# Spatial self-attention on one core: q and k biases as a row copied by PE, q/k product ahead of the second transposes, and the general path's DMAs on Pool's queue

## The chip, the cores and the metric

The kernel runs on one core of one Trainium2 chip. The time is the device microseconds of one execution; the profile's span is the part of it from the first to the last instruction. Before the change the median of three runs is 2447.41 us (2447.21 to 2447.56); the profiled execution took 2446.75 us and its span is 2445.0 us.

Engines are named as in the profile: PE multiplies matrices (PEld loads its weights), DVE and ACT do element-wise work, Pool (POOL) does a little arithmetic and issues DMAs, SP only issues DMAs. A "q" after a name (SPq, ACTq) is that engine's sequencer.

## What is computed

The input x is (4, 64, 64, 256) in float32: four images, 4096 positions each, 256 channels. Weights are Wq and Wk (256 x 128), Wv (256 x 256), with biases bq, bk (128 each), bv (256) and one scalar gamma.

```python
q = jnp.einsum('bwhc,cd->bwhd', x, Wq) + bq
k = jnp.einsum('bwhc,cd->bwhd', x, Wk) + bk
v = jnp.einsum('bwhc,cd->bwhd', x, Wv) + bv
pq = q.reshape(B, -1, N)          # N = 4096; the reshape mixes positions and channels
pk = k.reshape(B, -1, N)
pv = v.reshape(B, -1, N)
energy = jnp.einsum('bcn,bcm->bnm', pq, pk)
attention = jax.nn.softmax(energy, axis=-1)
out = jnp.einsum('bcm,bnm->bcn', pv, attention)
return gamma * out.reshape(B, W, H, C) + x
```

## The kernel before

The kernel handles one image after another. For each image it first projects, in sixteen blocks `i` of 256 rows of x, and then attends, in 128 steps `u`: sixteen groups `g` of 256 query columns, each against eight blocks `t` of key columns. All values are float32; where precision matters each factor is split into a rounded half and remainders (`halved`, `halve_v`, `halves`), and the products of the halves are summed.

**Projection** (class `Projection`, L102). `load` brings a block of x into one of three buffers by SP's queue (L82). `transposed` turns it on PE, four 128x128 transposes (L122), and ACT copies the result from PSUM to SBUF as `xts` (L128). `qk` multiplies it by the joined weights `wqk_sb`, four products with 256 columns, which the trace shows as eight passes (L135); DVE adds the bias row `bqk_sb`, which stands in all 128 partitions, and writes `qks` (L144). `v` does the same with `wv_sb` (L156), ACT adding the bias `bv` (L165). `project_qk` (L271) then stores q to a scratch tensor `qd` in device memory and writes the halves of k, `f` (ACT L263, then DVE L266), to a scratch tensor `kf`, both by Pool's queue (L275, L279). The attention reads both back (`qr` L303, `k` L314), which makes the reshape of the reference.

**Attention.** `energy` makes two products per key block, `sa` and `sb` (L330), and ACT takes their exponentials (L334). `join`, `upper` and `halves` form the three factors on DVE and ACT; `attend` sums `a` and `bb` over the key blocks (L383). The last column of `vh` and `vl` holds ones, so the sum of the exponentials comes along. `finish` scales, transposes back, adds x and stores by Pool (L420). `finish_last` does it for the last group in a shorter way and stores by SP (L464).

**No maximum is subtracted** before the exponentials. So the kernel checks all sums against bounds at the end (`inside`, L422): PE sums the verdicts of all partitions (`zp`, L449), DVE writes the flag `again` (L460), and all five engines load the flag and branch on it (the `tc.If`, L563). The code inside the If, the **general path**, computes everything once more with the maximum subtracted; for these inputs the flag is 0 and all engines jump over it. Its DMAs are all on SP's queue: loads of x through `load_x`, loads of `xr` (L651) and stores (L661). Pool has no instruction inside it. After the If every engine goes to the closing barriers, which stand under the launch's line in the profile (L688); SP waits there for all queues and engines.

**The order of the work** is written out by hand: inside `manual_schedule` the instructions stand on each engine in the order in which the Python code gives them, and a semaphore wait is put where an instruction needs another engine's or a DMA's result. A DMA counts up one of eight semaphores of its kind (SP's and ACT's share eight, Pool's have eight) taken in turn.

**The start**, around which most of the change lies. Pool makes the identity `ident` (L86) and issues, in this order: bq and bk to all 128 partitions (L91, L92, 64 KB each as written), wv (L94, 256 KB), the two halves of bv (L97) and gamma (L100). SP issues x_0, x_1 and x_2 (256 KB each). ACT loads its table, fills the columns of ones, and issues wq and wk (L223, L224, 128 KB each). PE keeps itself busy with products of ones (`wp`, L197), then follows the order at L486 to L494: transposes of x_0, two more products of ones (L492), transposes of x_1, the q/k product of block 0. The loop after it goes on with block `i`: transposes of block i + 1, q/k product of block i, v product of block i - 1.

PSUM banks for these first blocks are taken in turn from `energies` (four banks of `ps_s`), later from `outputs`. The buffers `qks` are two of the pool `work`, used in turn.

Of the kernel before, what the change touches and what calls it, by code (L numbers as in the profile page):

```python
# [9 lines left out]
F32 = mybir.dt.float32  # L10
# [10 lines left out]
def kernel(  # L21
# [36 lines left out]
    nc = tc.nc  # L58
    B, W, H, C = x.shape
    P = 128  # L60
    N = W * H
    C2 = C // 2
# [13 lines left out]
    xv, ov = columns(x, XB), columns(out, XB)  # L76

    const = ctx.enter_context(tc.tile_pool(name="const", bufs=1))

    def load_x(pool, b, g):  # L80
        t = pool.tile([P, 2, XB], F32, tag="x", name=f"x_{b}_{g}")
        nc.sync.dma_start(t, xv[b, g])  # L82
        return t

    ident = const.tile([P, P], F32, name="ident")
# [1 line left out]
    ones = const.tile([P, P], F32, name="ones")  # L87
    nc.vector.memset(ones, 1.0)
    wqk_sb = const.tile([P, KC, 2 * C2], F32, name="wqk_sb")
    bqk_sb = const.tile([P, 2 * C2], F32, name="bqk_sb")  # L90
    nc.gpsimd.dma_start(bqk_sb[:, :C2], bq.partition_broadcast(P))  # L91
    nc.gpsimd.dma_start(bqk_sb[:, C2:], bk.partition_broadcast(P))  # L92
    wv_sb = const.tile([P, KC, C], F32, name="wv_sb")
    nc.gpsimd.dma_start(wv_sb, wv.rearrange("(k p) e -> p k e", p=P))  # L94
    bv_sb = const.tile([P, KC], F32, name="bv_sb")
    for eh in range(KC):
        nc.gpsimd.dma_start(bv_sb[:, eh : eh + 1], bv[eh * P : (eh + 1) * P].unsqueeze(1))  # L97
    gam2 = const.tile([P, 2], F32, name="gam")
    gam, gam1 = gam2[:, :1], gam2[:, 1:]
    nc.gpsimd.dma_start(gam, gamma.partition_broadcast(P))  # L100

    class Projection:  # L102


        def __init__(self, b, xpool, psum, xt_out, qk_out, v_out):
            self.b, self.xpool, self.psum = b, xpool, psum
            self.xt_out, self.qk_out, self.v_out = xt_out, qk_out, v_out
            self.xs, self.xt = {}, {}

        def load(self, g):  # L110
            if g < NI and g not in self.xs:
                self.xs[g] = load_x(self.xpool, self.b, g)

        def transposed(self, i):

# [78 lines left out]
    with tc.tile_pool(name="ps_w", bufs=1, space=PSUM) as ps_w:  # L194
        wp = ps_w.tile([P, P], F32, name="wp")
# [3 lines left out]
    with ExitStack() as fast:  # L199
        fast.enter_context(tc.manual_schedule())  # L200
        pool = lambda name, bufs, **kw: fast.enter_context(
            tc.tile_pool(name=name, bufs=bufs, **kw)
        )
        xpool, xtpool, qkv = pool("xpool", 3), pool("xtpool", 3), pool("qkv", 1)
# [4 lines left out]
        work = pool("work", 2)  # L209
# [12 lines left out]
            nc.scalar.copy(t[:, :, C : C + 2], ones[:, : 2 * NM].rearrange("p (m t) -> p m t", t=2))  # L222
        nc.scalar.dma_start(wqk_sb[:, :, :C2], wq.rearrange("(k p) d -> p k d", p=P))  # L223
        nc.scalar.dma_start(wqk_sb[:, :, C2:], wk.rearrange("(k p) d -> p k d", p=P))  # L224

        images, qd, kf, units, loads, now = [], {}, {}, {}, {}, {}

# [43 lines left out]
        def project_qk(b, i):  # L271
            images[b].qk(i)
            x = now["qk"]
            for s in range(2):
                nc.gpsimd.dma_start(qd[b, i // 2 + NG // 2 * s][:, i % 2, :], x[:, s, :C2])  # L275
            f = kpool.tile([P, 2, 3, P], F32R, tag="f", name=f"f_{b}_{i}", bufs=2)
            for _ in halved(f, x[:, :, C2:]):
                pass
            nc.gpsimd.dma_start(kf[b, i // 2][:, i % 2], f.rearrange("p s j d -> p s (j d)"))  # L279
# [204 lines left out]
        for b in range(B):  # L484
            pr = images[b]
            if b == 0:  # L486
                now["banks"] = energies
                pr.transposed(0)

                wp = ps_t.tile([P, P], F32, tag="t", name="wp1")  # L490
                for _ in range(2):
                    nc.tensor.matmul(wp, ones, ones, start=True, stop=True)  # L492
                pr.transposed(1)
                project_qk(b, 0)  # L494
            for i in range(1, NI):
                if i == 3:
                    now["banks"] = outputs
                if i + 1 < NI:
                    pr.transposed(i + 1)
                while i == 1 and active:  # L500
                    proceed()
                begin(b, i)
                project_qk(b, i)
                if i == NI - 1:
                    halves(b, 0)
                project_v(b, i - 1)
                proceed()
            project_v(b, NI - 1)
            for u in range(STEPS):
                g, t = divmod(u, NU)  # L510
                ahead = u + LOOK
                if ahead // NU + 1 < NG and ahead % NU == 3:
                    load_q(b, ahead // NU + 1)
                if u == STEPS - NU and b + 1 < B:
                    image(b + 1)
                if u >= STEPS - 3 and b + 1 < B:
                    now["banks"] = energies
                    if u == STEPS - 3:
                        images[b + 1].load(0)
                    elif u == STEPS - 2:  # L520
                        images[b + 1].transposed(0)
                if t == NU - 3:
                    loads[b, "x", g] = load_x(xpool, b, g)


                beside = []
                if ahead // NU + 1 < NG and ahead % NU == 5:
                    beside.append(halve_q(b, ahead // NU + 1))
                if u in (1, 3):
                    beside.append(halve_v(b, NI - 2 + u // 2))  # L530
                for k in range(2):
                    if ahead < STEPS:
                        energy(b, ahead, k)
                    if k == 0:
                        for forms in beside:
                            next(forms)
                    if k == 0 and u + 2 < STEPS:
                        join(b, u + 2)
                        upper(b, u + 2)
                load_k(b, ahead + 2)  # L540
                proceed()
                if u + 1 < STEPS:
                    halves(b, u + 1)
                for forms in beside:
                    next(forms)
                attend(b, u)
                if (b, u) == (B - 1, STEPS - 1):
                    finish_last(b, g, loads.pop((b, "x", g)))
                elif t == NU - 1:
                    start(finish(b, g, now["o"], now["bb"], loads.pop((b, "x", g))))  # L550
                proceed()
            if b + 1 < B:
                proceed()
                images[b + 1].transposed(1)
                proceed()
                project_qk(b + 1, 0)
# [6 lines left out]
    with tc.If(nc.values_load(again[0:1, 0:1]) > 0), ExitStack() as general:  # L563
# [8 lines left out]
        for b in range(B):  # L572
# [8 lines left out]
                lambda i: xtpool.tile([P, KC, 2, P], F32, tag="xt", name=f"gxt_{b}_{i}"),  # L581
                lambda i: ((pq[:, i::NI, :], 0), (pk[:, i::NI, :], C2)),
                lambda i: (pvT[:, 2 * i : 2 * i + 2, :], bv_sb, 1.0),
            )
            for i in range(NI):
                pr.transposed(i)
# [2 lines left out]
            for g in range(NG):  # L589
# [58 lines left out]
                                stop=(2 * t + h == NM - 1),  # L648
                            )
                xr = xpool.tile([P, 2, NB], F32, tag="xr", name=f"gxr_{b}_{g}")  # L650
                nc.sync.dma_start(xr, xg[b, g])  # L651
                nc.vector.tensor_tensor(ssum[:, 0, :], ssum[:, 0, :], ssum[:, 1, :], ALU.add)
                zb = ps_t.tile([P, NB], F32, tag="t", name=f"gzb_{b}_{g}")
                nc.tensor.matmul(zb, ones, ssum[:, 0, :], start=True, stop=True)
# [2 lines left out]
                for s in range(2):  # L657
                    y = work.tile([P, NB], F32, tag="y", name=f"gy_{b}_{g}_{s}")
                    nc.vector.scalar_tensor_tensor(y, r, gam, acc[s], ALU.mult, ALU.mult)
                    nc.vector.tensor_tensor(xr[:, s, :], xr[:, s, :], y, ALU.add)  # L660
                nc.sync.dma_start(og[b, g], xr)  # L661


# [28 lines left out]
```

## Time and profile before

| what | value | from |
|---|---|---|
| time, median of 3 | 2447.41 us | the times |
| span | 2445.0 us | the page's head |
| PE busy | 2434.4 us (100%) | the page, part 1 |
| PEld, DVE, ACT, POOL busy | 98%, 86%, 74%, 17% | the page, part 1 |
| chain that ended last: PE | 99% of the span | the page, part 4 |
| q/k products (L135), v products (L156) | 5% of the chain each | the page, part 4 |
| DMA traffic | 498.92 MB, mean 204 GB/s | the page, part 2 |
| x loads, issue to landing (median) | 3.9 us | the page, part 6 |
| wq, wk | 3.4 and 5.9 us | the answer on DMAs |
| bq, bk as broadcasts | 5.0 and 5.4 us | the answer on DMAs |
| wv | 6.3 us | the page, part 6 |
| bv (two loads), gamma | 5.6 and 5.1 us | the answer on DMAs |
| last output store by SP | 3.5 us | the page, part 6 |

How to read it: an engine's share of busy time says how full it is over the whole span, and a busy PE says little about whether its passes are at their peak. The chain of waits is followed from the last instruction back, so its shares say which engine's speed set the end. Stages are read from the table of windows, which gives the busy time of each engine between two moments; single instructions from the timeline, whose bracket says how long the engine stood idle ahead of an instruction and who released it. Times are microseconds from the span's start.

### The profile page before, as it was taken

The numbers are of one execution on the slowest core, as the hardware profiler recorded it, in microseconds if no ns is written. First come the engines' busy times: TensorE is split into PE (matmuls) and PEld (weight loads), VectorE is DVE, ScalarE is ACT, GpSimd is POOL, SyncE is SP. The second block draws the span as 40 slices with busy tenths as digits, with TensorE's granted clock in tenths as the row PEclk, the third lists the DMA queues.
The fourth block names the chain that finished last, engine by engine and source line by source line (L and its number), as shares of the span: only waits on it lengthen the run. The fifth ranks groups of instructions, "written<-read, shape, count | busy, mean of one in ns | idle before, by whom it ended". The sixth has DMA issues, their size and how long they took to land.

```text
span 2445.0 us, 50042 instructions
## 1 busy us (share of the span) xinstructions
PE 2434.4 (100%) x19988; PEld 2403.8 (98%) x19988; DVE 2100.4 (86%) x2318; ACT 1797.5 (74%) x3201; POOL 425.8 (17%) x781
## 2 busy tenths in 40 slices
PE   9999999999999999999999999999999999999998
PEld 8999999999899999999989999999998999999998
DVE  5988888888698888888869888888886988888887
ACT  5777777777677777777667777777766777777775
POOL 4211111111411111111141111111114111111110
PEclk9999999999999999999999999999999999999999
DMA  7766666665776666666477666666647766666663
GB/s 233 225 201 213 203 207 202 203 214 156 232 225 197 210 204 207 209 197 212 145 241 229 202 201 207 205 209 201 205 143 245 230 204 198 210 204 209 207 202 114
DMA packets 137407, 498.92 MB, mean 204 GB/s; under 512 B 15536, under 2 KB 57264, under 8 KB 137168
## 3 DMA queue, kind: packets, MB, share of 16 engines
q0 software_dynamic: 92320, 453.17, 59.8%
q1 hardware_dynamic: 44304, 42.22, 5.5%
q8 instruction: 160, 2.62, 0.4%
q14 instruction: 79, 0.65, 0.1%
q10 hardware_dynamic: 544, 0.26, 0.0%
HBM read 445.25 MB, written 50.33 MB: 203 GB/s over the span
## 4 chain that ended last, share of the span: by engine, by line
PE 99%; DMA 0%; DVE 0%; SPq 0%; issue 0%
PE a L383 40%; PE bb L383 19%; PE sa L330 19%; PE sb L330 10%; PE qk L135 5%; PE v L156 5%; PE xt L122 1%; PE ot L415 1%; DMA x<-in_x_dram 0%; SPq L82 0%; DVE o L452 0%; PE ot L457 0%; DVE x L463 0%; PE zp L449 0%; DVE r L441 0%
## 5 line engine op out<-in xcount | busy, mean ns | idle before, releaser
L334 ACT ACTIVATE x<-sa 128x512 f32<-128x512 f32 x1024 | 614.2, 600 | 507.6 <-PE sa L330 505.4
L344 DVE TENSOR_TENSOR x<-x,y 128x1024 f32<-128x1024 f32 x512 | 627.0, 1225 | 228.2 <-ACT y L334 228.2
L330 PE MATMUL sa<-q,k 128*128 128x256 f32 x4096 | 733.2, 279 | 0.0
L355 DVE TENSOR_TENSOR l<-x,h 128x1024 fp32r<-128x1024 f32 x512 | 624.0, 1219 | 0.0
L358 DVE SCALAR_TENSOR_TENSOR d<-h,x 128x1024 fp32r<-128x1024 f32 x512 | 624.0, 1219 | 0.0
L330 PEld LDWEIGHTS sa<-q,k 128*128 128x128 f32 x4096 | 617.9, 188 | 0.4
L334 ACT ACTIVATE y<-sb 128x512 f32<-128x512 f32 x1024 | 615.1, 601 | 0.0
L383 PE MATMUL a<-vh,h 128*128 128x258 f32 x4096 | 574.3, 282 | 0.0
L383 PE MATMUL a<-vl,l 128*128 128x258 f32 x4096 | 571.9, 282 | 0.0
L330 PE MATMUL sb<-q,k 128*128 128x256 f32 x2048 | 566.2, 276 | 0.0
L383 PE MATMUL bb<-vd,d 128*128 128x256 f32 x4096 | 556.3, 278 | 0.0
L314 POOL DMA_DIRECT2D k<-kf x512 | 279.8, 546 | 1566.6 <-PE sb L330 1541.7
L349 ACT ACTIVATE h<-x 128x1024 fp32r<-128x1024 f32 x512 | 543.9, 1062 | 9.1 <-DVE x L344 8.4
L383 PEld LDWEIGHTS a<-vl,l 128*128 128x128 f32 x4096 | 524.6, 189 | 0.0
L383 PEld LDWEIGHTS a<-vh,h 128*128 128x128 f32 x4096 | 522.7, 189 | 0.0
L383 PEld LDWEIGHTS bb<-vd,d 128*128 128x128 f32 x4096 | 513.7, 188 | 0.0
L330 PEld LDWEIGHTS sb<-q,k 128*128 128x128 f32 x2048 | 384.9, 188 | 0.1
L135 PE MATMUL qk<-wqk_sb,xts 128*128 128x256 f32 x512 | 121.1, 379 | 0.0
L156 PE MATMUL v<-xts,wv_sb 128*128 128x256 f32 x512 | 120.3, 379 | 0.0
L156 PEld LDWEIGHTS v<-xts,wv_sb 128*128 128x128 f32 x512 | 97.3, 190 | 13.2
L135 PEld LDWEIGHTS qk<-wqk_sb,xts 128*128 128x128 f32 x512 | 92.3, 190 | 10.0
L275 POOL DMA_DIRECT2D qd<-qks x128 | 69.4, 550 | 179.5 <-DVE qks L144 170.3
(60 smaller groups left out, 868.6 us busy)
## 6 DMA issues: line engine op xcount, KB each, us to landing
k<-kf POOLq DMA_DIRECT2D x512, 768.0 KB, 4.7
x<-in_x_dram SPq DMA_DIRECT2D x128, 256.0 KB, 3.9
kf<-f POOLq DMA_DIRECT2D x64, 384.0 KB, 3.7
out_dram<-x POOLq DMA_DIRECT2D x63, 256.0 KB, 2.5
qd<-qks POOLq DMA_DIRECT2D x128, 64.0 KB, 2.9
qr<-qd SPq DMA_DIRECT2D x64, 128.0 KB, 3.6
wv_sb<-in_L_conv_Wv_dram POOLq DMA_DIRECT2D x1, 256.0 KB, 6.3
out_dram<-x SPq DMA_DIRECT2D x1, 256.0 KB, 3.5
```

What stands on the lines that cost most here:

```text
L122: nc.tensor.transpose(tp[:, k, s, :], self.xs[i][:, s, k * P : (k + 1) * P], ident,)
L135: nc.tensor.matmul(qk[:, s, :], self.xt[i][:, k, s, :], wqk_sb[:, k, :], start=(k == 0), stop=(k == KC - 1),)
L156: nc.tensor.matmul(vp[:, eh, :], wv_sb[:, k, eh * P : (eh + 1) * P], self.xt[i][:, k].rearrange("p s a -> p (s a)"), start=(k == 0), stop= ...
L275: nc.gpsimd.dma_start(qd[b, i // 2 + NG // 2 * s][:, i % 2, :], x[:, s, :C2])
L314: nc.gpsimd.dma_start(t.rearrange("p (i s) f d -> p i s (f d)", s=2), kf[b, u % NU])
L330: nc.tensor.matmul(to[:, i], kt[:, 2 * k + i, f, :], q[:, f], start=first, stop=last)
L334: nc.scalar.activation(to[:, 2 * k : 2 * k + 2, :], sp.rearrange("p i j d -> p i (j d)"), AF.Exp, scale=scale,)
L344: nc.vector.tensor_tensor(x, x, y, ALU.mult)
L349: nc.scalar.activation(h, units[b, u], AF.Identity, scale=UPPER)
L355: nc.vector.tensor_tensor(l, x, h.bitcast(F32), ALU.subtract)
L358: nc.vector.scalar_tensor_tensor(d, h.bitcast(F32), 1.0 + E, x, ALU.mult, ALU.subtract)
L383: nc.tensor.matmul(out_, left[:, i, j * P : (j + 1) * P], right[:, m, : out_.shape[1]], start=(t == i == 0 and (left is h or left is d and ...
```

## The change

Three edits, of which two concern the start and one the end.

1. **Biases of q and k.** They are no longer copied to all partitions by DMAs on Pool's queue. ACT's queue loads each as a row into one partition (0.5 KB each, after wq and wk), in a buffer of `qks` (`bqk_row`). PE multiplies a column of ones by the row (`bqk_all`, in the bank of `bb`), which puts the row in all partitions, and DVE copies the result to `bqk_sb`. One of the two products of ones at L492 goes. On Pool's queue bv and gamma now come first and wv last.
2. **Order of the first products.** The q/k product of block 0 comes ahead of the transposes of block 1.
3. **General path.** Its DMAs are issued by Pool instead of SP, so SP has none inside the If. The loads of the fast path stay on SP.

```diff
-    def load_x(pool, b, g):
+    def load_x(pool, b, g, by=nc.sync):
         t = pool.tile([P, 2, XB], F32, tag="x", name=f"x_{b}_{g}")
-        nc.sync.dma_start(t, xv[b, g])
+        by.dma_start(t, xv[b, g])
         return t
...
     bqk_sb = const.tile([P, 2 * C2], F32, name="bqk_sb")
-    nc.gpsimd.dma_start(bqk_sb[:, :C2], bq.partition_broadcast(P))
-    nc.gpsimd.dma_start(bqk_sb[:, C2:], bk.partition_broadcast(P))
     wv_sb = const.tile([P, KC, C], F32, name="wv_sb")
-    nc.gpsimd.dma_start(wv_sb, wv.rearrange("(k p) e -> p k e", p=P))
     bv_sb = const.tile([P, KC], F32, name="bv_sb")
     for eh in range(KC):
         nc.gpsimd.dma_start(bv_sb[:, eh : eh + 1], bv[eh * P : (eh + 1) * P].unsqueeze(1))
     gam2 = const.tile([P, 2], F32, name="gam")
     gam, gam1 = gam2[:, :1], gam2[:, 1:]
     nc.gpsimd.dma_start(gam, gamma.partition_broadcast(P))
+    nc.gpsimd.dma_start(wv_sb, wv.rearrange("(k p) e -> p k e", p=P))
...
+        row = work.tile([P, 2, 2 * C2], F32, tag="qk", name="bqk_row")[:1, 0, :]
+        nc.scalar.dma_start(row[:, :C2], bq.unsqueeze(0))
+        nc.scalar.dma_start(row[:, C2:], bk.unsqueeze(0))
...
                 pr.transposed(0)
 
                 wp = ps_t.tile([P, P], F32, tag="t", name="wp1")
-                for _ in range(2):
-                    nc.tensor.matmul(wp, ones, ones, start=True, stop=True)
+                nc.tensor.matmul(wp, ones, ones, start=True, stop=True)
+                bp = ps_o.tile([P, 2 * C2], F32, tag="bb", name="bqk_all")
+                nc.tensor.matmul(bp, ones[:1, :], row, start=True, stop=True)
+                nc.vector.tensor_copy(bqk_sb, bp)
+                project_qk(b, 0)
                 pr.transposed(1)
-                project_qk(b, 0)
...
                 lambda i: (pvT[:, 2 * i : 2 * i + 2, :], bv_sb, 1.0),
+                nc.gpsimd,
             )
...
-                nc.sync.dma_start(xr, xg[b, g])
+                nc.gpsimd.dma_start(xr, xg[b, g])
...
-                nc.sync.dma_start(og[b, g], xr)
+                nc.gpsimd.dma_start(og[b, g], xr)
```

The class `Projection` takes the issuing engine as an argument and hands it to `load_x`; the fast path leaves it at SP.

More of the change, by code (lines that the diff above doesn't have):

```diff
@@ L100, with __init__ @@
     nc.gpsimd.dma_start(gam, gamma.partition_broadcast(P))
+    nc.gpsimd.dma_start(wv_sb, wv.rearrange("(k p) e -> p k e", p=P))
     class Projection:
-        def __init__(self, b, xpool, psum, xt_out, qk_out, v_out):
-            self.b, self.xpool, self.psum = b, xpool, psum
+        def __init__(self, b, xpool, psum, xt_out, qk_out, v_out, by=nc.sync):
+            self.b, self.xpool, self.psum, self.by = b, xpool, psum, by
             self.xt_out, self.qk_out, self.v_out = xt_out, qk_out, v_out
@@ L111, in load @@
             if g < NI and g not in self.xs:
-                self.xs[g] = load_x(self.xpool, self.b, g)
+                self.xs[g] = load_x(self.xpool, self.b, g, self.by)
         def transposed(self, i):
```

## The prediction

> **What bounds the kernel now.** I read the page's chain first (PE 99% of the span), then cut the span into stages in the table of windows. Columns: window, its length, then busy us (and count) of PE, PEld, DVE, ACT, POOL, then clock, DMA share, GB/s.
>
> ```profile
> 4.40:7.07 2.67, 1.34 (x9) 1.18 (x9) 0.00 (x0) 0.59 (x1) 0.80 (x2) 1.00 0.86 237
> 7.07:2434.20 2427.13, 2427.13 (x19950) 2397.62 (x19951) 2097.11 (x2302) 1794.26 (x3195) 421.58 (x769) 1.00 0.66 205
> 2434.20:2438.10 3.90, 2.62 (x19) 1.91 (x17) 3.17 (x15) 0.95 (x2) 0.00 (x0) 1.00 0.00 0
> 2438.10:2445.00 6.90, 0.00 (x0) 0.00 (x0) 0.00 (x0) 0.00 (x0) 0.00 (x0) 0.55 0.15 50
> ```
>
> From 7.07 to 2434.20 PE has no idle at all: 2427.13 of 2427.13 us. The change removes no PE work there, so it can win only in the first 7.07 us and after 2434.20, where the last 6.90 us hold no arithmetic. Next, the timeline of the start, PE alone (start, duration, line, operation), then ACT alone:
>
> ```profile
> 4.51 0.89 PE L122 MATMUL xt<-ident,x 128*128 128x128 f32 x4
> 5.24 0.61 PE L492 MATMUL wp<-ones 128*128 128x128 f32 x4
> 7.07 0.66 PE L122 MATMUL xt<-ident,x 128*128 128x128 f32 x4 [1.22 <-DMA x<-in_x_dram]
> 7.58 1.97 PE L135 MATMUL qk<-wqk_sb,xts 128*128 128x256 f32 x8
> 9.38 0.60 PE L122 MATMUL xt<-ident,x 128*128 128x128 f32 x4
> ```
> ```profile
> 5.44 0.59 ACT L128 COPY xts<-xt 128x512 f32<-128x512 f32 x1 [3.02 <-PE xt L122]
> 7.76 0.59 ACT L128 COPY xts<-xt 128x512 f32<-128x512 f32 x1 [1.74 <-PE xt L122]
> 10.30 0.42 ACT L263 ACTIVATE f<-qks 128x256 fp32r<-128x256 f32 x1 [1.96 <-DVE qks L144]
> 10.63 0.57 ACT L128 COPY xts<-xt 128x512 f32<-128x512 f32 x1
> ```
>
> PE stands 1.22 us for x_1, though xts_0 has been ready since 5.44 + 0.59 = 6.03; the first q/k product starts at 7.58 and the second at 9.81. Why is x_1 late? Issued at 1.48, it landed 5.55 us later by the chain of waits; x_0 took 3.4. The DMA view of 3.0 to 4.3 us (packets, MB, share of 16 engines' time):
>
> ```profile
> q1 hardware_dynamic: 134, 0.12, 29.9%
> q0 software_dynamic: 15, 0.05, 43.1%
> ```
>
> Of 16 x 1.3 = 20.8 us of engine time, Pool's queue q0 took 9.0 us for 15 packets, 0.60 us each; its head is the two bias broadcasts (64 KB each). A packet of x on q1 took 6.2/134 = 0.046 us. Then the end, by the If's line L563 (engine, operation, count, duration in ns, start):
>
> ```profile
> L563 SPq EVENT_SEMAPHORE  x8: 17/17/17, 2442.3 to 2442.8; - x8
> ...
> L563 POOLq COMPARE_BRANCH  x1: 45/45/45, 2437.2 to 2437.2; - x1
> ...
> L563 PEldq COMPARE_BRANCH  x1: 3770/3770/3770, 2437.7 to 2437.7; - x1
> ...
> L563 SPq COMPARE_BRANCH  x1: 45/45/45, 2439.7 to 2439.7; - x1
> ...
> L563 PEldq EVENT_SEMAPHORE  x1: 51/51/51, 2441.6 to 2441.6; - x1
> ```
>
> SP branches at 2439.7 and does its next thing at 2442.3: 2.6 us. ACT (2437.2 to 2439.9) and DVE (2438.2 to 2441.1) show the same gap, 2.7 and 2.9; PE 3.8. Pool, which has nothing inside the If, is at its final drain at 2437.4, 0.2 us after branching. SP is last: eight waits to 2442.8, twelve more from 2442.9, its drain at 2443.6 (line L688), and the closing barriers take 1.4 us to 2445.0.
>
> **What the Trainium skill says.** "Runtime: NRT & Kernel Launch", Instruction fetch mechanics: a taken branch whose target lies outside the two pages held forces a fetch. The trace agrees: 2.6 to 3.8 us on the four engines that jump over code, 0.2 on the one that doesn't. "DMA: Bandwidth & Descriptors", Queues, rings and completion order: each DMA engine takes the queues in turn, a packet at a time. So a 0.60 us packet delays x and the weights; the window above fits, but shows no packet-by-packet order. "TensorE: Matmul & The Clock Gate", What's actually happening: PE is slow until busy for some 3.4 us; the trace agrees (0.24 us a pass from 1.05, 0.11 from about 5), and that warm-up stays.
>
> **The change, part by part.**
>
> *Broadcasts out, rows in.* Two 64 KB loads go from Pool's queue; 2 x 16 packets of 4 KB, an estimate from their size, at 0.60 us are 19 us of engine time, or 1.2 us of all sixteen. Two rows of 0.5 KB go onto ACT's queue, behind wk (issued 1.51, 0.68 us long), so at about 2.2 and 2.8. The queue's only measure is its own: wq landed 3.4 us after issue, wk 5.9, at 7.4. Bounds for wk in the new kernel: 5.3 (x_0, wq, x_1, wk are 768 KB; at the 300 GB/s of the good stretches 2.5 us from the first packet at 2.25, plus 0.5 to complete) and 7.4 (nothing gained). I take about 6.0, 7.4 less the 1.2 us and a little of the thin traffic after 4.3 us. The rows come with wk, or soon after.
>
> *PE's copy.* One warm-up matmul goes (0.3 us), one 128x256 product comes: two passes of 0.215 (L135: 1.73 us per 8), 0.43 us. The new order is wp, rows' product, qk_0, xt_1, xt_2, qk_1. The product stands ahead of qk_0, so it adds a wait: all of PE is queued behind the rows. If they land by 5.5 it ends near 6.0 and costs nothing, since qk_0 waits for xts_0 until 6.03. DVE's copy of the 128x256 sum, some 0.4 us, is done before qk_0 ends: nothing.
>
> *qk_0 ahead of xt_1.* qk_0 starts at S = 6.03 + 0.1 = 6.15 instead of 7.58, 1.4 us earlier. But it pays back. In the new order ACT holds f_0 ahead of xts_1, and f_0 waits for qk_0's bias add on DVE. From qk_0's start: 1.97 its own, 0.03 + 0.69 DVE, 0.03 to f_0, 0.33 until the next copy starts (10.30 to 10.63), 0.57 that copy, 0.1 to PE: 3.7 us until qk_1, with only xt_1 and xt_2 (0.44 each) to fill the 1.9 us after qk_0. Before, 9.81 - 7.58 = 2.23. So qk_1 starts at 6.15 + 3.7 = 9.87 against 9.81: **the start gives +0.06 us**, nothing. With wk at 7.4 it is 7.5 + 3.7 = 11.2: +1.4.
>
> *Pool's other loads.* wv is issued last, at about 3.4 instead of 2.85; at the 6.3 us it took it lands by 10.2, v_0 needs it at 11.6: nothing. bv and gamma come earlier and are first used at 13.5 (v's bias): nothing.
>
> *General path by Pool.* It isn't run here (again is 0), but SP's code inside the If goes and the compiled program leaves SP only its branches there. So SP's 2.6 us should become Pool's 0.2, and its eight waits go with them. What then ends last? The output store, issued at 2438.00, lands 3.5 us later, at 2441.5, and PE's semaphore is set at 2441.65; SP's final waits include both. Three more waits at 0.06 us and the drain: about 2441.85 against 2443.6: **the end gives -1.75 us**. Pool now jumps over code (2437.2 + 2.7 = 2439.9, five waits, 2440.4): hidden behind PE. No more than 2.1 us can be had, as the store itself stands.
>
> *Steady part.* The waits of all later instructions are on the same producers as before; only semaphore numbers and the parity of the qk work buffers shift. PE is without idle: nothing.
>
> Sum: +0.06 - 1.75 = -1.7; 2447.4 - 1.7 = **2445.7 us** (-0.07%).
>
> **The rivals.**
>
> *A, as above*, with start within +-0.5: 2445.7. Chance 0.55.
>
> *B, wk stays late.* Thin traffic from 4.3 to 5.75 us (100 to 155 GB/s, by quarters) outlasts most of the broadcasts, so something else may hold wk. Start +0.5 to +1.4, end -1.75: 2446.2 to 2447.1, say 2446.8. Chance 0.22.
>
> *C, slower: the rows gate PE and the end wins little.* Small loads behind large ones took 5.1 to 5.8 us here (bv, gamma). A row issued at 2.8 and 5.4 long lands at 8.2; product to 8.7, qk_1 at 12.4: +2.6. With -1.75 that is 2448.3; with PE's fetch slowed by Pool's and an end of -0.5, 2449.5. Against it: bv and gamma were on the broadcasts' queue. Chance 0.13.
>
> *D, the start wins too.* ACT passes xts_1 sooner than the sum says, or x_0 comes earlier: -0.5, and -2.1 at the end: 2444.8. Chance 0.10.
>
> **How the numbers follow.** A is the likeliest: 2445.7. The range takes D's 2444.8 below, and B with the better part of C above, 2447.9; left out are worse cases of C and surprises below D, some 15 in 100. The bound of 0.2% is 4.9 us. The biggest win that the sums allow is 2.6 us, and the worst of C is a loss of 2.1; only a disturbed steady part reaches further. Faster 0.03, same 0.95, slower 0.02.
>
> **What would show it.** Right: SP's drain near 2441.9 less the shift of the start, no gap of 2.5 us after SP's branch, PE's semaphore as last; q0's slow packets gone at 3 to 5 us; qk_0 at about 6.15; PE idle about 0.8 us ahead of qk_1, with xts_1 behind f_0 on ACT; PE without idle afterwards. Wrong: qk_0 waiting beyond 6.5 for wk or the rows, SP still fetching, the barriers waiting for Pool, or idle PE in the middle.

## The result and the profile after

| | before | after |
|---|---|---|
| time, median of 6 runs each | 2447.19 us | 2455.43 us |
| ratio after/before, 95% interval | | 1.0033 [1.0021, 1.0046] |
| span of the profiled run | 2445.0 us | 2453.1 us |
| q/k product of block 0: start, length | 7.58, 1.97 | 7.28, 3.30 |
| q/k product of block 1: start | 9.81 | 12.28 |
| the flag's product (`zp` on PE): start | 2436.08 | 2439.08 |
| from there to the end of the span | 8.92 us | 14.02 us |

The kernel became 8.2 us slower, where 1.7 us less was forecast. The last two rows divide the 8.1 us of span: 3.0 us were lost before the flag's product, 5.1 us behind it. `zp` is a good mark to divide at, since the same few instructions precede it in both kernels. Its piece of the chain of waits (start, us, what), before and after:

```profile
2436.08 0.37 PE zp L449 x2
2439.08 0.37 PE zp L451 x2
```

The windows of the kernel after, laid as those of before (window, length, busy us and count of PE, PEld, DVE, ACT, POOL, clock, DMA share, GB/s):

```profile
4.40:7.07 2.67, 1.24 (x8) 0.98 (x8) 0.00 (x0) 0.58 (x1) 0.22 (x1) 1.00 1.01 325
7.07:20.00 12.93, 12.47 (x57) 10.41 (x56) 5.22 (x10) 4.17 (x10) 3.69 (x8) 0.87 0.48 155
20.00:2437.20 2417.20, 2416.92 (x19898) 2388.47 (x19896) 2091.41 (x2293) 1788.58 (x3186) 416.42 (x761) 1.00 0.65 205
2437.20:2441.10 3.90, 2.62 (x19) 1.91 (x17) 3.16 (x15) 0.95 (x2) 0.00 (x0) 1.00 0.00 0
2441.10:2453.10 12.00, 0.00 (x0) 0.00 (x0) 0.00 (x0) 0.00 (x0) 0.00 (x0) 0.52 0.09 29
```

Three things are to be seen. The stretch without arithmetic at the end grew from 6.90 to 12.00 us. From 7.07 to 20.00 PE's granted clock has a mean of 0.87, where it was 1.00. And the middle is nearly as it was: PE idles 0.28 us in 2417.20.

**The start.** PE's timeline of the kernel after (start, duration, line, operation; the bracket is idle time and its releaser), then ACT's:

```profile
4.50 0.63 PE L120 MATMUL xt<-ident,x 128*128 128x128 f32 x4
4.97 0.39 PE L493 MATMUL wp<-ones 128*128 128x128 f32 x2
6.68 0.67 PE L495 MATMUL bqk_all<-bqk_row,ones 1*128 1x256 f32 x2 [1.33 <-DMA bqk_row<-in_L_conv_bk_dram]
7.28 3.30 PE L133 MATMUL qk<-wqk_sb,xts 128*128 128x256 f32 x8
10.37 1.46 PE L120 MATMUL xt<-ident,x 128*128 128x128 f32 x8
12.28 1.99 PE L133 MATMUL qk<-wqk_sb,xts 128*128 128x256 f32 x8 [0.46 <-ACT xts L126]
```
```profile
5.17 0.58 ACT L126 COPY xts<-xt 128x512 f32<-128x512 f32 x1 [2.75 <-PE xt L120]
11.34 0.42 ACT L265 ACTIVATE f<-qks 128x256 fp32r<-128x256 f32 x1 [5.59 <-DVE qks L142]
11.66 1.05 ACT L126 COPY xts<-xt 128x512 f32<-128x512 f32 x2
```

`xts_0` is ready at 5.75, even earlier than assumed, and wk has landed (4.9 us after its issue, at 6.4) when it is wanted. But PE waits 1.33 us for the row of bk. Two things are behind the loss. First, the row: the chain of waits of the kernel after, in order of time, ends its first leg with it:

```profile
2.96 3.59 DMA bqk_row<-in_L_conv_bk_dram
6.55 0.14 issue
6.68 0.67 PE bqk_all L495 x2
```

A load of 0.5 KB takes 3.59 us; it was issued last, behind x_0, wq, x_1 and wk (an experiment below puts it first). The traffic of 3.0 to 4.3 us by queue (packets, MB, share of 16 engines' time) shows that this isn't the broadcasts' doing any more:

```profile
q1 hardware_dynamic: 178, 0.17, 40.8%
q0 software_dynamic: 22, 0.00, 1.3%
```

Pool's queue had 43.1% of this time and now has 1.3%; between 4.40 and 7.07 the loads flow at 325 GB/s instead of 237, and x_1 no longer makes PE wait. The removal did what it was for. The second thing is the q/k product itself, which takes 3.30 us instead of 1.97. Windows of half a microsecond of the kernel after show why (the clock is the third figure from the end):

```profile
7.00:7.50 0.50, 0.50 (x3) 0.22 (x2) 0.11 (x1) 0.00 (x0) 0.03 (x2) 1.00 1.01 330
7.50:8.00 0.50, 0.50 (x3) 0.45 (x3) 0.31 (x1) 0.00 (x0) 0.20 (x1) 0.81 0.41 131
8.00:8.50 0.50, 0.50 (x3) 0.41 (x2) 0.00 (x0) 0.00 (x0) 0.00 (x0) 0.50 0.03 8
...
11.00:11.50 0.50, 0.50 (x6) 0.50 (x5) 0.31 (x1) 0.16 (x1) 0.00 (x0) 0.78 0.00 0
```

A mean of 0.81 over half a microsecond puts the fall to half at about 7.8, and 0.78 the return at about 11.2: some 3.4 us at half speed, just as the first product runs.

**The end.** The If's line in the kernel after (L567; engine, operation, count, ns, start), then the closing line of the launch (L693; DRAIN and EVENT_SEMAPHORE with min/median/max ns and the first and last start), then the closing line of the kernel before (L688). DRAIN and INC_SWDGE_SEM are the profile's names; no statement of kernel.py asks for either here.

```profile
L567 POOLq EVENT_SEMAPHORE  x4: 17/43/43, 2443.5 to 2443.8; - x4
...
L567 POOLq COMPARE_BRANCH  x1: 45/45/45, 2440.2 to 2440.2; - x1
...
L567 SPq COMPARE_BRANCH  x1: 50/50/50, 2442.7 to 2442.7; - x1
...
L567 POOLq INC_SWDGE_SEM  x1: 1787/1787/1787, 2443.8 to 2443.8; - x1
```
```profile
L693 SPq EVENT_SEMAPHORE  x14: 17/28/28, 2445.6 to 2453.0; - x14
L693 POOLq DRAIN  x3: 46/107/6602, 2445.7 to 2452.8; - x3
L693 SPq DRAIN  x3: 7/7/7, 2446.3 to 2452.5; - x3
```
```profile
L688 POOLq DRAIN  x3: 46/107/6683, 2437.4 to 2444.7; - x3
L688 SPq DRAIN  x3: 7/7/13, 2443.6 to 2444.4; - x3
```

Read the drains together. In the kernel before Pool's first drain starts at 2437.4 and takes 6.683 us, to 2444.1; SP's is at 2443.6. So Pool ended last already, by 0.5 us, and the barriers led to 2445.0. In the kernel after Pool branches at 2440.2, jumps over the code of the general path (3.3 us until its four waits at 2443.5), runs an INC_SWDGE_SEM of 1.787 us that was not there before, and only then, at 2445.7, starts the drain, which takes 6.602 us again, to 2452.3. SP is at its drain at 2446.3, 6.0 us before that.

Counted from the flag's product, SP comes to its drain after 7.2 us, where it took 7.5 before. Why so little, if it has no code to jump over any more? It branches at 2442.7, but its closing waits begin only at 2445.6, which is when Pool's INC_SWDGE_SEM ends (2443.8 + 1.787); the view of waits puts the 2.8 us between down to a DMA of Pool's queue. In the later versions with the general path on Pool the two times agree as well (2447.1 and 2447.2 where INC_SWDGE_SEM is long again), so SP most likely waits for that instruction.

### The profile page after: what moved, and what is told of

Its sections match the earlier page's. It is cut to its first block, busy times and chain, and to the rows that moved or that the text cites. A ratio compares the mean times of both kernels' runs of the same rounds, so it can differ in the third digit from the quotient of the medians.

```text
span 2453.1 us, 50041 instructions
## 1 busy us (share of the span) xinstructions
PE 2436.6 (99%) x19988; PEld 2404.8 (98%) x19988; DVE 2100.0 (86%) x2319; ACT 1796.0 (73%) x3201; POOL 423.5 (17%) x779
## 4 chain that ended last, share of the span: by engine, by line
PE 98%; ACT 0%; DMA 0%; issue 0%; DVE 0%; POOL 0%; ACTq 0%; POOLq 0%; DVEq 0%
PE a L385 40%; PE bb L385 19%; PE sa L332 19%; PE sb L332 9%; PE qk L133 4%; PE v L154 4%; PE ot L417 1%; PE xt L120 1%; DMA kf<-f 0%; ACT v L163 0%; DMA bqk_row<-in_L_conv_bk_dram 0%; DVE qks L142 0%; ACT vh L294 0%; ACT f L265 0%; DVE f L268 0%
```

## The experiments

The theory after this reading: Pool's closing drain has a fixed length from where it starts and sets the end, so every delay of it is paid in full; and at the start the rows gate PE and the clock drops in the stall. Rivals: the end's loss belongs to Pool's far branch alone; the drain waits for something that other engines do; the new order costs the start by itself. The chips of the experiments ran the kernel before at 2449.5 to 2449.8 us, with more spread (2447.3 to 2452.6) than the first (2446.7 to 2447.6), so every version's time is compared with the kernel before on the same chip. The kernel before was profiled on the first chip only, and each version once. "End" is from the flag's product to the end of the span, as in the table (before: 8.92 us).

### The edits apart

```diff
# general path by Pool, in the kernel before (and x's loads in the If, by an argument)
-                nc.sync.dma_start(xr, xg[b, g])
+                nc.gpsimd.dma_start(xr, xg[b, g])
...
-                nc.sync.dma_start(og[b, g], xr)
+                nc.gpsimd.dma_start(og[b, g], xr)
# start only: the changed kernel with these two, and x's loads in the If, on nc.sync
# general path by ACT: as the first, with nc.scalar
```

> The kernel before with the general path's DMAs moved to Pool, nothing else. Theory 1 (Pool's closing drain takes a fixed 6.6 us wherever it starts, and the skip path now puts a far branch and a 1.8 us INC_SWDGE_SEM ahead of it): the drain starts near 2442.7 instead of 2437.4, span +5.1 us, time about 2452.3. Theory 2 (Pool's drain merely waits for the other engines, and the loss of the changed kernel at the end comes from something that its start brings): SP's saved branch shows, time about 2445.5; with theory 2 the drain's 6.6 us would shrink.

> The changed kernel with the general path's DMAs back on SP: the start's edits alone. If the two losses are independent: the end as in the kernel before (10.8 us from PE's last product for attend to the span's end), the start +2.5 to 3.0 us, time about 2449.9. If the end's loss needs the start's edits: about 2455.

> The kernel before with the general path's DMAs on ACT's queue: SP has nothing inside the If, and Pool has nothing either. Theory 1 (the fixed drain of Pool set the end of the kernel before too: 2437.4 + 6.68 = 2444.1): span unchanged within 0.3 us, time about 2447.0, although SP's drain comes near 2441.9. Rival, as the prediction had it (SP's branch and eight waits set the end): -1.75 us, time about 2445.4.

General path on Pool alone: 2455.94 us against 2449.68, 1.0025 [1.0016, 1.0035], end 13.43 us. Pool's drain starts 5.9 us after the flag's product (2441.27) and is as long as before:

```profile
L689 POOLq DRAIN  x3: 46/107/6683, 2447.2 to 2454.4; - x3
```

This one edit loses some 6.3 us on that chip, of which the profiles put 13.43 - 8.92 = 4.5 at the end. The rest lies ahead of the flag's product, where nothing was edited: x_1 and wk came later (a first product at 10.12, 3.75 long). In the three versions that keep the broadcasts and have the general path on Pool wk landed 7.7 to 8.5 us after its issue, in the eight others with broadcasts 5.9 to 7.4; what the edit has to do with it stays open.

Start alone: 2450.96, 1.0002 [0.9993, 1.0011], end 9.03; its rows made PE wait 2.3 us and its first product took 3.78. So the 3.0 us of the first chip don't show in this comparison, because the kernel before is itself over 2 us slower here.

General path on ACT: 2449.82, 1.0000 [0.9991, 1.0009], end 8.85. This is the test of the forecast's gain. SP branched at 2442.6 and did its first wait at 2442.8, so its gap of 2.6 us did become 0.2, as forecast, and yet nothing was gained. Its closing line says why:

```profile
L689 POOLq DRAIN  x3: 46/107/6683, 2440.3 to 2447.5; - x3
L689 SPq DRAIN  x3: 7/7/7, 2445.4 to 2447.2; - x3
```

Pool's drain, 2440.3 + 6.7 = 2447.0, ends 1.6 us after SP's began.

### Is the drain's length fixed?

```diff
# the last output store by Pool, in the kernel before
-            nc.sync.dma_start(ov[b, g], xr)
+            nc.gpsimd.dma_start(ov[b, g], xr)
```

> The kernel before with the last output store (L464) issued by Pool instead of SP, nothing else. Pool can then load the flag only after the store is issued, about 2.1 us later than before. Theory 1 (Pool's closing drain takes a fixed 6.6 us and sets the end): the end moves by the same 2.1 us, time +2.1 us. Theory 2 (the drain ends when the others arrive): the end unchanged, since SP's path gets shorter, not longer. If the drain grows beyond 6.7 us with a store in flight: more than +2.1.

The store delays Pool's drain, and moves work off SP. Measured: 2450.81 us against 2449.66, 1.0006 [0.9997, 1.0015], in time inconclusive; end 10.56 us, 1.64 more than before. The closing line of this version:

```profile
L688 POOLq DRAIN  x3: 46/107/6769, 2440.0 to 2447.3; - x3
L688 SPq DRAIN  x3: 7/7/13, 2443.0 to 2447.0; - x3
```

SP, the last of the other engines, is at its drain at 2443.0, 3.8 us before Pool's long one ends, so that drain doesn't simply end when the others arrive. Pool's drain started 2.96 us after the flag's product instead of 1.32, 1.6 later (2.1 was expected), and the end moved by the same 1.6. Six to seven microseconds that follow their start wherever it is put.

The length isn't quite the same in all versions, and the differences go with the edits: 6.602 us wherever Pool doesn't issue the two broadcasts (the kernel after and the start's edits alone, for example), 6.683 wherever it does (the kernel before, the general path on Pool or on ACT), 6.769 here, with one store more. So the length seems to go with what Pool was given to issue, even 2430 us earlier; what the drain does in that time no view shows.

### Paying the drain early

```diff
                 if (b, u) == (B - 1, STEPS - 1):
+                    nc.gpsimd.drain()
                     finish_last(b, g, loads.pop((b, "x", g)))
```

One version has this with the general path on ACT, one is the changed kernel with this line only.

> The kernel before with a drain of Pool right after its last DMA (near 2421 us, 15 us ahead of the flag) and the general path's DMAs on ACT. Theory 1 (the drain is a settling of Pool's DMA queue, paid once, and then it closes the span): the early drain takes 6.6 us under PE's work, the closing one 0.1 to 0.2 us, and SP's path becomes the last: from PE's product for the flag to the span's end 7.8 us instead of 8.9, time -1.1 us. Rival (the closing drain costs 6.6 us whatever went before): end unchanged.

> The changed kernel as it is, general path on Pool, with a drain of Pool right after its last DMA. Theory (the 6.6 us belong to the DMAs issued before, not to the semaphore increments of the skip path): the closing drain is short, and the end is Pool's far branch and INC_SWDGE_SEM, then the barriers: about 7.8 to 8.3 us from the flag's product instead of 14.0, time -6 us against the changed kernel. Rival (INC_SWDGE_SEM makes a drain long again): end still 13.4 to 14.0 us.

On ACT: 2449.89 against 2449.48, 1.0002 [0.9993, 1.0010], end 8.45, 0.65 more than expected (in the last barrier step PE came to its second drain only at 2446.6, 1.6 us after SP's last). The changed kernel: 2448.05, 0.9995 [0.9986, 1.0003], end 6.25 instead of 14.02, and below the 7.8 to 8.3 that were expected. The early drain's line, the If's and the closing line of the changed kernel with it:

```profile
L552 POOLq DRAIN  x1: 7321/7321/7321, 2419.5 to 2419.5; - x1
```
```profile
L568 POOLq INC_SWDGE_SEM  x1: 181/181/181, 2444.2 to 2444.2; - x1
```
```profile
L694 POOLq DRAIN  x3: 34/51/107, 2444.4 to 2446.0; - x3
```

The long drain lies at 2419.5, where PE has work for another 20 us. After it INC_SWDGE_SEM takes 181 ns instead of 1787, and the closing drains 34 to 107 ns instead of 6602: 7.8 us go from the end, and the time is within the noise that of the kernel before. Pool's far branch is still there (2441.2, its waits at 2443.9), so that alone wasn't the loss.

### The start: rows, order, clock

```diff
# warm: the start's edits with seven products of ones instead of one
-                nc.tensor.matmul(wp, ones, ones, start=True, stop=True)
+                for _ in range(7):
+                    nc.tensor.matmul(wp, ones, ones, start=True, stop=True)
# order only: the kernel before with
-                pr.transposed(1)
                 project_qk(b, 0)
+                pr.transposed(1)
# rows only: the start's edits with the old order
# rows first: the start's edits with the rows issued ahead of wq and wk
```

> The start's edits alone, as in the run before this, with seven products of ones ahead of the rows' product instead of one (six more, 0.22 us each at full clock, which fill PE's 1.3 us wait for the rows). If PE's idle stretch took its clock down: qk_0 takes 1.97 instead of 3.30 us and qk_1 starts 1.3 us earlier, time about 2448.6. If the slow qk_0 has another cause (the weights still landing, PSUM): qk_0 stays at 3.3 us and the time at about 2449.9 or a little more.

> The kernel before with the first q/k product ahead of the transposes of block 1; biases as broadcasts, general path on SP. Theory (the order pays back on ACT what it wins, and wk, held up by the broadcasts and by x_1 and x_2, gates qk_0): PE stands idle from xt_0 until wk lands, near 7.5 to 9, so one long idle stretch instead of x_1's; qk_1 starts 3.7 us after qk_0, later than in the kernel before by 1 to 2 us[...]. Rival (the order by itself is a gain and the rows spoil it): qk_1 earlier than before.

> The start's edits without the new order: rows' product, then the transposes of block 1, then qk_0; general path on SP. Theory (the rows land last of all early loads and PE stands behind them): PE idle from 5.4 until the rows land at 6.5 to 7.4; then xt_1 without a wait, qk_0 0.5 us later, qk_1 2.2 us after qk_0 with no wait for xts_1: against the start's edits together qk_1 comes 1.0 us earlier (no 1.5 us of payback, 0.5 us for xt_1). Rival (the payback of the order is nothing on the chip): qk_1 0.4 us later than with the order.

> The start's edits, general path on SP, with the two rows ahead of wq and wk on ACT's queue instead of behind them. Theory (the rows are late only because they queue behind 256 KB of weights in a saturated DMA): rows' product near 5.0 to 5.5 without a wait, then qk_0 waits for wk, which is issued 1.2 us later and lands at about 7 to 8: PE's idle stretch only moves from the rows to wk, qk_1 within 0.5 us of where it was. Rival (the rows alone were the gate): qk_0 at about 6.2, qk_1 at about 9.9.

| version | first q/k product: start, length | second: start | time, ratio |
|---|---|---|---|
| start alone | 8.67, 3.78 | 14.15 | 2450.96, 1.0002 [0.9993, 1.0011] |
| warm | 7.51, 1.99 | 11.21 | 2449.45, 1.0000 [0.9991, 1.0009] |
| order only | 9.00, 3.75 | 14.46 | 2451.05, 1.0006 [0.9998, 1.0015] |
| rows only | 8.81, 3.62 | 13.08 | 2449.41, 0.9998 [0.9989, 1.0007] |
| rows first | 7.30, 3.65 | 12.65 | 2450.16, 1.0002 [0.9994, 1.0011] |

The ratios settle nothing here; the timelines do. PE's timeline of the warm version:

```profile
5.23 1.73 PE L494 MATMUL wp<-ones 128*128 128x128 f32 x14
6.89 0.69 PE L496 MATMUL bqk_all<-bqk_row,ones 1*128 1x256 f32 x2
7.51 1.99 PE L133 MATMUL qk<-wqk_sb,xts 128*128 128x256 f32 x8
11.21 1.99 PE L133 MATMUL qk<-wqk_sb,xts 128*128 128x256 f32 x8 [0.83 <-ACT xts L126]
```

With the wait filled by products whose result nobody reads, the clock stays at 1.00 and the product takes 1.99 us. Its 12 runs also lie closer (2448.3 to 2450.0) than the 12 of "start alone" (2448.3 to 2451.7). So the stall, by way of the clock, is what lengthened it. From one q/k product to the next it is 11.21 - 7.51 = 3.7 us, to the tenth what the forecast worked out for the new order at full clock. "Rows first" moves the wait: the rows' product runs at 5.12 without one, and the next line of PE's timeline reads

```profile
7.30 3.65 PE L133 MATMUL qk<-wqk_sb,xts 128*128 128x256 f32 x8 [1.48 <-DMA wqk_sb<-in_L_conv_Wk_dram]
```

Whichever load is last gates PE, and the clock falls either way. "Start alone" and "rows only" differ in the order, and both ran this stretch at half speed: from the first product to the second 5.5 and 4.3 us, so the payback of the new order costs 1.2 there, by one profile of each. "Order only" is gated by wk, for 3.53 us, and is no earlier for the new order. In "rows only" the record of the clock shows 1.00 throughout, yet a transpose or a product of ones took at least 421 ns from PE's first to the one at 12.9, where "start alone" shows 275 at 4.9: in that execution PE did not come to full speed before 12.9, and the length of the passes is the safer sign.

### A fill in the kernel before, and versions built from the findings

```diff
# fill: the kernel before with
-                for _ in range(2):
+                for _ in range(8):
                     nc.tensor.matmul(wp, ones, ones, start=True, stop=True)
# all, ACT: rows, old order, eight products of ones, early drain, general path on ACT
# all, Pool: the same with the general path on Pool
```

> The kernel before with eight products of ones instead of two in PE's wait for x_1 (L492), nothing else. If PE's idle stretch costs a window at half clock in part of the runs: qk_0 takes 1.9 us always, the slow part of the runs is gone, median 1 to 1.7 us below the kernel before on a chip where that has slow runs, nothing on one where it has none. If the spread has another cause: no change, or +0.3 us where x_1 lands before the products end.

> Rows of the biases by PE, eight products of ones while they come, the order of the kernel before (x_1's transposes, then qk_0), general path's DMAs on ACT, Pool's drain early. If the effects add: qk_1 at about 10.2 with the clock never down, end 7.8 us from the flag's product: 2 to 3 us below the kernel before on the same chip. If the rows' gate eats what the clock wins: -1.1 us.

> The changed kernel with the old order of the first products, eight products of ones instead of one, and the early drain: as the version with the general path on ACT, but on Pool. Theory: end of 6.3 us, start at full clock (first q/k product about 8.4 us, 1.9 us long, second 10.5), time about 1.2 us below the version with ACT, some 0.15% below the kernel before. Rival (ends do not add to starts): no better than that version, 0.10% below the kernel before.

Fill: 2447.94 us against 2449.48, 0.9995 [0.9987, 1.0004]; its 13 runs lie within 1.4 us, the 41 of before beside it within 4.6. Since the fill takes 1.5 us off the median, the kernel before probably has the slow clock in most of its runs on these chips. All, ACT: 2446.85, 0.9990 [0.9981, 0.9998], end 7.44. All, Pool, on another chip: 2446.18 against 2449.78, 0.9985 [0.9979, 0.9992], end 6.43. It is 0.15% below the kernel before, clear of the noise, and so below both kernels. PE's timeline of its start:

```profile
7.26 0.69 PE L496 MATMUL bqk_all<-bqk_row,ones 1*128 1x256 f32 x2
8.38 1.89 PE L133 MATMUL qk<-wqk_sb,xts 128*128 128x256 f32 x8
```

No wait ahead of the rows' product, and a first product of 1.89 us.

### What the third edit is worth once the drain is paid

```diff
# drain, SP: the kernel before with the early drain
# drain, Pool: the same with the general path on Pool
# each again with the fill of eight products of ones
```

> The kernel before with Pool's drain put ahead of the last block's finishing, and nothing else; the general path stays on SP. From the start of the flag's product on PE to the end of the span: theory (Pool's closing drain is a fixed 6.6 us that hides the worth of everything else at the end): with it gone SP's own drain is last, 7.5 us after the flag's product as in the kernel before, plus 0.9 us of barriers: 8.4 us, 0.5 us less than before. Rival (where the general path stands does not matter once the drain is early): 6.3 us, as in the changed kernel with the early drain.

> The same early drain in the kernel before, with the general path's DMAs by Pool, and nothing of the start. Theory (the third edit removes SP's far branch and eight waits, and what it adds on Pool is short once the drain is paid): 6.3 us from the flag's product to the end, about 2.1 us less than with the path on SP, and time 2.1 us lower than that kernel. Rival (the better end of the changed kernel with early drain came from its start): about 8.4 us, no difference.

> The kernel before with eight products of ones instead of two at the start, the early drain, and the general path by Pool; no rows, old order. It differs from the early drain with the path on Pool only by the six products, which also shift where PE's later code stands. Theory (the 3.2 us that PE took there between its last wait inside the If and its drain is a fetch of code, and goes when PE's code is shifted): end of 6.3 to 6.6 us from the flag's product. Rival (that stall belongs to the path on Pool without the rows): 9.6 us again. Start in both at full clock: first q/k product about 8.4 us, 1.9 us long. Against the best version so far it tells whether the rows are needed: theory that fill and drain are enough, 0.1 to 0.15% below the kernel before.

> The same with the general path on SP. Theory (the third edit removes SP's fetch and eight waits, about 2 us, once the drain is early): end of 8.4 to 9.0 us, time about 2 us above the version with the path on Pool. Rival (the third edit is worth nothing): the same time as that version.

| version | end | time, ratio |
|---|---|---|
| drain, SP | 8.95 us | 2449.98, 1.0002 [0.9993, 1.0010] |
| drain, Pool | 9.65 us | 2451.38, 1.0007 [0.9998, 1.0015] |
| fill, drain, SP | 8.60 us | 2447.86, 0.9992 [0.9984, 1.0000] |
| fill, drain, Pool | 6.58 us | 2446.79, 0.9989 [0.9982, 0.9995] |

The second was expected at 6.3 us and missed by 3.4. Its If's line and closing line show where, and the queues of 2446.5 to 2449.9 us (packets, MB, share) what moved meanwhile:

```profile
L564 PEldq EVENT_SEMAPHORE  x1: 51/51/51, 2446.5 to 2446.5; - x1
```
```profile
L690 PEldq DRAIN  x2: 8/8/8, 2449.8 to 2450.2; - x2
```
```profile
q8 instruction: 1, 0.02, 2.3%
q14 instruction: 1, 0.01, 1.0%
```

PE stood 3.2 us between its last wait inside the If and its drain, the very next thing, and nothing but instructions was loaded meanwhile. The general path on Pool alone, which has the same program for PE, shows the stall too, on another chip (wait at 2446.5, drain at 2450.0), hidden there behind Pool's drain. With six more products at PE's start, which shift the rest of its code and touch nothing at the end, PE's drain follows its wait at once and the end is 6.58:

```profile
L564 PEldq EVENT_SEMAPHORE  x1: 51/51/51, 2443.9 to 2443.9; - x1
...
L690 PEldq DRAIN  x2: 8/8/8, 2444.0 to 2444.5; - x2
```

So the stall goes with where PE's code stands, by these three executions, and most likely is a fetch; which packet was PE's the trace doesn't say. With that stall out of the way the third edit is worth 8.60 - 6.58 = 2.0 us at the end. In time the two differ by 1.1 us only: in the profiled run of the Pool version, which took the median time, the second q/k product started 0.8 us later (11.90 against 11.07, a wait of 0.82 us for wk). The first of the table was expected at 8.4 and gave 8.95: SP's own path, 7.45 us to its drain, then 1.5 us of barriers, in which PE came to its second drain 0.9 us after SP's; so the early drain alone wins nothing while SP is last.

## Why the prediction was wrong

**What bounds the kernel: held.** The change could act only ahead of the steady part and behind it, and did, but for 0.5 us that come back below.

**General path by Pool, -1.75 us: wrong, +5.1 us; this step failed.** It read "Pool ... is at its final drain at 2437.4" as Pool being done, and asked "What then ends last?" of PE and the store alone. That drain is 6.683 us of work that ended at 2444.1, after SP's. Two things were wrong. One: no gain of SP could show behind that drain, as the version on ACT proved (SP's gap gone, end 8.85). Two: "Pool now jumps over code (...): hidden behind PE" put 3.2 us (2437.2 to 2440.4) ahead of a drain that nothing hides. Measured: 3.3 us until the waits, 0.3 for these, 1.8 for INC_SWDGE_SEM (no term of the forecast), and the unchanged drain; the drain started at 2445.7, 6.6 us after the flag's product, instead of 1.3. That is 5.3; 0.1 comes back in the shorter drain and 0.1 in the barriers, 5.1.

SP's own drain was forecast near 2441.9, which is 5.8 us after the flag's product of before. It came after 7.2 us, where before took 7.5: a gain of 0.3, as its waits began only when INC_SWDGE_SEM ended. Once the early drain makes that instruction short and PE doesn't stall, the term for SP has about the size forecast (2.0 us at the end). In the change as it stands it was neither on the path nor that large. "The barriers waiting for Pool" stood among the forecast's signs of being wrong, but no sum had a term for it.

SP, ACT, DVE and PE were followed through the If one by one; Pool was not, as it "has nothing inside the If". The page of the Trainium skill that was cited there for the far branches ("Runtime: NRT & Kernel Launch", Instruction fetch mechanics) fits the four engines that jump over code in the kernel after too: 2.7 us on ACT, 3.1 on DVE, 3.4 on PE and 3.3 on Pool. The skill's "VectorE: DVE Perf Modes", The DRAIN you can't avoid, puts closing drains at a constant of about 12 ns on all engines; SP's, ACT's, DVE's and PE's took 7 to 17 ns here, Pool's 6.6 us, and the measurement decides.

**"The rows come with wk, or soon after": right as an event, but put at nothing in the sum.** wk landed at 6.4 (6.0 was forecast), in time, and the broadcasts' slow packets went; the rows landed at 6.55, where 5.5 was the latest that would have cost nothing. The forecast's own figures said as much: rows at 6.0 or later, 0.1 us to the product and 0.43 for it make a start of 6.5 at the earliest, and the sum went on with 6.15. (Of the bound of 5.3 for wk, 0.5 us "to complete" come from no line shown; nothing rests on them.) Rival C named the event (the rows gate PE) with 0.13, and put the product's end at 8.7; it was 7.35. This term alone is 7.28 - 6.15 = 1.1 us on the first product.

**The clock, "that warm-up stays": the second failing term.** The warm-up itself was as before, but the clock didn't stay up behind it. The product of block 0 was costed at its 1.97 us of before and took 3.30; from it to the second product 5.00 us passed instead of 3.72 (+1.28), as the stall of 1.33 us was followed by 3.4 us at half clock. The length of the stall alone doesn't decide: the kernel before had one of 1.22 us without such a fall, the version with the store on Pool one of 1.72 us (first product 1.89), while with the general path on ACT one of 2.00 us was followed by a product of 3.31, with the same old start. The Trainium skill, "TensorE: Matmul & The Clock Gate", What's actually happening, says that the window of about 3.4 us runs freely, so that a change of clock depends on where in it the work falls. The length of 3.4 us agrees, and where the clock stayed down longer it was twice that, 6.8 us ("start alone", "order only"); that 1.3 us of idleness were enough here is the measurement's.

**The new order, "+0.06 us": right as worked out, 3.7 us between the products at full clock.** Together 1.13 + 1.28 + 0.06 make the 2.47 us from 9.81 to 12.28. The other 0.5 us up to the flag's product come later. Between the second q/k product and the flag's product the profiles of all versions took 2426.2 to 2427.5 us, with 2426.3 in the kernel before. In the kernel after 0.28 us of it is one wait of PE for DVE; the chain of waits leads from there back to 2.7 us in which Pool stood idle and for which the trace names no cause, but the kernel before has such a stretch too, of 4.2 us, and PE doesn't wait there. So the cause of the 0.5 us stays open, and no run was made for it.

**The rivals and the range.** None had an end that grows. The range covered the unknown of SP's gain between -0.5 and -2.1, not a new bound; rival C's slower side came from the start alone.

## What to carry to other kernels

Before moving DMAs to another engine at the end of a kernel, find every engine's closing drain with its length, not its start: the engine that "only drains" may be the one that ends last, and what is put ahead of that drain is paid in full. A fixed cost of that kind can be moved under other work, here by one explicit drain 20 us earlier, and only then do the gains of the other engines show. At the start, a new small load behind large ones is the last to land, and the stall that it makes can cost a second time through TensorE's clock; in the six versions with unread products in the gap it stayed up.

## What the runs showed of the hardware

- Pool's first drain after its DMAs took 6.60 to 6.77 us at the end and 7.32 to 7.41 us 20 us earlier, in both places 0.08 us less where Pool issued two loads fewer at the start, although Pool's last DMA had been issued 21.8 us before the drain in the kernel before (2415.6, 2437.4). The drains after it took 34 to 107 ns.
- INC_SWDGE_SEM on Pool took 1.79 to 1.81 us ahead of that drain and 0.18 us after it; SP's closing waits began as it ended.
- PE's clock fell to half for 3.4 us behind stalls of 1.33, 1.48, 1.66, 2.00 and 2.76 us and for 6.8 us behind others of 2.24, 2.30, 3.38 and 3.53 us, but not at all behind stalls of 1.22, 1.69 and 1.72 us.
- A load of 0.5 KB behind four large ones took 3.6 to 4.5 us from issue to landing (3.59 in the kernel after, 4.46 with the start alone).
- With six products more at PE's start, 2430 us ahead, a stall of 3.2 us in PE's last step was gone.
